# Chunked linear attention inside a one-core mixture block: chunks of 128 tokens made into chunks of 64

## The chip, the core and the metric

The kernel runs on one core of a Trainium2 chip. The metric is device time in microseconds of one launch, the median of several runs. Five engines work beside each other, each through its own queue in order: the PE (TensorE, matrix products; its weight loads have rows of their own, PEld), DVE (VectorE), ACT (ScalarE), POOL (GpSimd) and SP, which issues most transfers. PSUM, where matmul results land, has eight banks of 128 partitions by 512 float32 columns.

## The reference, cut to what matters

The input is 8 sequences (b = 0 to 7) of 512 tokens and 512 features. After a layer norm, one branch is a linear attention with 16 heads of 32 features, the other a mixture of 16 experts with 4 per token; the output is `x + attention * silu(mixture)`. In the attention each head has a decay `lam`, and the reference goes through the tokens in chunks of C = 128:

```
scores  = (q_i @ k_i^T) * D            # D[t,s] = exp(lam*(t-s)) for t >= s, else 0
o_intra = scores @ v_i
o_inter = (q_i * decay_q) @ S          # S: the state before the chunk, 32x32 a head
S       = lam_C * S + (k_i * decay_k)^T @ v_i
o       = o_intra + o_inter
```

Then o is multiplied with a sigmoid gate, each head is normalised by its root mean square, and a 512 by 512 product with Wo follows. The result of the recurrence does not depend on the size of the chunk.

## The kernel before, in words

All of it is float32. Heads come in four groups (g = 0 to 3) of four, so that a group fills 128 partitions. For one (b, g) the attention does this, with the lines of the profile:

- `key` and `query` (L659 products of 4 matmuls by 512 columns; ACT's Silu L669; four DVE operations L671 to L675 for the rotation) leave kT and qT, features on partitions, 512 tokens on columns. The key product goes to PSUM tag "m" (one bank), the query product to tag "d" (two banks).
- `by_token` transposes kT to tokens on partitions (L691, three chunks), into the one kept bank "k", and ACT scales it by the decay of the token (L696, four operations) into `kd`.
- `scores` makes the chunks' key-value products (L714, 12 matmuls of 128 rows by 32 columns, four column strips of the array beside each other), then the scores (L725, 16 matmuls of 32 rows, four row strips beside each other, each head in a bank of tag "a", 512 columns). DVE runs the state recurrence, multiplies qT by the decay into `qd` (L744), and masks the scores (L750, four operations of 512 columns) into `sc`.
- `output` adds the inter products and the intra products (L772, 16 matmuls, four column strips) in one bank of tag "d"; DVE multiplies it into the gate (L776).

The recurrence has two forms. For b below 2 it is three small DVE operations (L738, L740), and the inter products are 12 matmuls of 32 by 32 (L766). From b = 2 on it is one DVE scan over three states (L729); ACT copies the four heads' states into the diagonal blocks of a zeroed 128 by 128 tile (`blocked`, L734, four copies), and the inter products are 3 full matmuls (L761).

A float32 matmul has two weight loads and two matmul records in the trace, so 16 matmuls are "x32".

The order around it is written out by hand in `sequence`: for each g, scores(g); key(g+2) or, for g of 2 and 3, the value products of the next sequence, value(b+1, 2(g-2)); by_token(g+1); projections of the sequence before (L817, tag "d"); query(g+2) or value(b+1, 1); then output(g). After output(3): gate_2 of the next sequence (L645, four banks "a"), value(b+1, 3), `squares` (ACT L783 squares each group, the PE sums them, L786), key and query of the next sequence, `normed` (L805, L810). Value products (L615, copied out by ACT at L619) use bank "m" for even t and "d" for odd t. The `on_pe` blocks keep the PE in the order in which the program is written; other engines are ordered by the scheduler. In the first stage `along` puts pieces of the router and of the shared expert between these steps: share_1 writes its gate product to bank "m" (L355), share_2 its third tile (L371). From b = 2 on `advance` puts steps of the mixture between them: gathers and adds on POOL, and DVE operations L1354, L1358 and L1381, which wait for POOL in DVE's queue.

Scratch tiles: `sc` has four buffers, `kd` and `qd` have one each; the four squares use the buffers of `sc`.

Of the kernel before, what the change touches and what calls it, by code (L numbers as in the profile page):

```python
# [10 lines left out]
F32 = mybir.dt.float32  # L11
# [11 lines left out]
G, HG = 4, 4  # L23
C = 128
NC = N // C
NT = B * NC
KC = D // P
E, F, TOPK = 16, 128, 4
# [25 lines left out]
def shape_constants():  # L54

    f = np.float32
    c = {}
    lam = -(f(2.0) ** (f(-8.0) * (np.arange(H, dtype=f) + f(1.0)) / f(H))).astype(f)
    i = np.arange(C, dtype=f)
    diff = i[None, :] - i[:, None]  # L60
    dec = np.exp(lam[None, :, None] * np.maximum(diff, f(0.0))[:, None, :])
    c["dmask"] = np.where(diff[:, None, :] >= 0, dec, f(0.0))
    dq = np.exp(lam[:, None] * (i[None, :] + f(1.0)))
    c["dq"] = np.repeat(dq.reshape(G, HG, 1, C), HD, axis=2).reshape(G, P, C).transpose(1, 0, 2)
    c["dk"] = np.exp(lam[None, :] * (f(C) - f(1.0) - i[:, None]))
    lc = np.exp(lam * f(C))
    c["lamc"] = np.repeat(lc.reshape(G, HG, 1), HD, axis=2).reshape(G, P).T

    c["carry"] = np.tile(c["lamc"][:, :, None, None] * (np.arange(NC - 1) > 0), (1, 1, HD, 1))
    half = HD // 2  # L70
    theta = (f(BASE) ** (f(-2.0) * np.arange(half, dtype=f) / f(HD))).astype(f)
    ang = (np.arange(N, dtype=f)[None, :] * theta[:, None]).astype(f)
    c["cos"] = np.tile(np.cos(ang), (2 * HG, 1))
    c["sin"] = np.tile(np.concatenate([-np.sin(ang), np.sin(ang)], axis=0), (HG, 1))
    c["ident"] = np.eye(P)


    sel = np.zeros((P, H - HG + Q))
    exp = np.zeros((H, G, P))
    for g in range(G):  # L80
        for j in range(HG):
            sel[j * HD : (j + 1) * HD, H - HG + j] = 1.0 / HD
            exp[g * HG + j, g, j * HD : (j + 1) * HD] = 1.0
    c["sel"] = sel

    c["tri"] = np.triu(np.ones((P, P)), 1) - 1.0
    c["iota_e"] = np.tile(np.arange(E), (P, 1))
    c["reset"] = np.tile((np.arange(NT) > 0)[None], (P, E)).reshape(P, E * NT)
    out = {k: np.ascontiguousarray(v.reshape(P, -1), dtype=f) for k, v in c.items()}
    out["exp"] = exp.reshape(H, D).astype(f)  # L90
    out["iota_b"] = (np.arange(P, dtype=f)[:, None] // Q * NBQ + np.arange(NBQ, dtype=f)).astype(f)
    out["token"] = (
        np.arange(NT)[None, :] * P + np.arange(P)[:, None] - B * N // 2).astype(np.float32)
    return out
# [3 lines left out]
def tile_block(ctx: ExitStack, tc: tile.TileContext, a: dict, out: bass.AP):  # L98
# [80 lines left out]
    cos = load(const, "cos", [P, N])  # L179
    sin = load(const, "sin", [P, N])  # L180
    wq = load_w(const, "wq")
    dk = load(const, "dk", [P, H])
    lamc = load(const, "lamc", [P, G])
    dq = load(const, "dq", [P, G, C])
    dmask = load(const, "dmask", [P, H, C])
    sel = load(const, "sel", [P, H - HG + Q])
    nw = load(const, "nw", [P, G])
    wo = load_w(const, "wo")
# [415 lines left out]

    between = [lambda: None]

    kept, carry, blocked = [], [], []

    def value(b, t):
        if t == 0:  # L610
# [73 lines left out]
    def by_token(b, g):  # L684

        if not kept:
            kept.append(bank("k", f"pk_{b}_{g}"))
        pk = kept[0]
        with on_pe():
            for c in range(NC - 1):  # L690
                nc.tensor.transpose(  # L691
                    pk[:, c * P : (c + 1) * P], kT_of[g][:, c * C : (c + 1) * C], ident)
        kd = scr[0].tile([P, NC - 1, HG, HD], F32, tag="kd", name=f"kd_{b}_{g}")
        by_chunk = pk[:, : (NC - 1) * P].rearrange("p (c h d) -> p c h d", c=NC - 1, d=HD)
        for j in range(HG):
            nc.scalar.activation(  # L696
                kd[:, :, j, :], by_chunk[:, :, j, :], AF.Copy,
                scale=dk[:, g * HG + j : g * HG + j + 1])
        kd_of[g] = pk[:, (NC - 1) * P :], kd

    masked = []

    def scores(b, g):

        pkv, kd = kd_of.pop(g)
        states = pkv[:, : (NC - 1) * HD].rearrange(
            "p (e c) -> p c e" if carry else "p (c e) -> p c e", e=HD)
        with on_pe():  # L710
            for c in range(NC - 1):
                for j in range(HG):
                    h = g * HG + j
                    nc.tensor.matmul(  # L714
                        states[j * HD : (j + 1) * HD, c, :], lhsT=kd[:, c, j, :],
                        rhs=v_of[b][:, c, h * HD : (h + 1) * HD], start=True, stop=True)
        kT, qT = kT_of.pop(g), qT_of.pop(g)
        sc_of[g] = []
        pss = [bank("a", f"ps_{b}_{g}_{j}") for j in range(HG)]
        with on_pe():  # L720
            for c in range(NC):
                cs = slice(c * C, (c + 1) * C)
                for j in range(HG):
                    hs = slice(j * HD, (j + 1) * HD)
                    nc.tensor.matmul(  # L725
                        pss[j][:, cs], lhsT=kT[hs, cs], rhs=qT[hs, cs], start=True, stop=True)
        st = scr[0].tile([P, (NC - 1) * HD], F32, tag="state", name=f"state_{b}_{g}")
        if carry:
            nc.vector.tensor_tensor_scan(  # L729
                st, carry[0][:, g, :], pkv[:, : (NC - 1) * HD], 0.0, ALU.mult, ALU.add)  # L730
            st_of[g] = blocked[g % 2]
            for j in range(HG):
                hs = slice(j * HD, (j + 1) * HD)
                nc.scalar.copy(  # L734
                    st_of[g][hs, :, hs], st[hs].rearrange("p (e c) -> p c e", e=HD))
        else:
            st_of[g] = st = st.rearrange("p (c e) -> p c e", e=HD)
            nc.vector.tensor_copy(st[:, 0], states[:, 0])  # L738
            for c in range(1, NC - 1):
                nc.vector.scalar_tensor_tensor(  # L740
                    st[:, c], st[:, c - 1], lamc[:, g : g + 1], states[:, c],
                    ALU.mult, ALU.add)
        qd = scr[0].tile([P, NC - 1, C], F32, tag="qd", name=f"qd_{b}_{g}")
        nc.vector.tensor_tensor(  # L744
            qd, qT[:, C:].rearrange("p (c t) -> p c t", t=C),
            dq[:, g].unsqueeze(1).to_broadcast([P, NC - 1, C]), ALU.mult)
        qd_of[g] = qd
        for j in range(HG):
            s = scr[0].tile([P, NC, C], F32, tag="sc", name=f"sc_{b}_{g}_{j}", bufs=4)
            masked[:] = [nc.vector.tensor_tensor(  # L750
                s, pss[j].rearrange("p (c t) -> p c t", t=C),
                dmask[:, g * HG + j].unsqueeze(1).to_broadcast([P, NC, C]), ALU.mult).ins]
            sc_of[g].append(s)

    def output(b, g):
        po = bank("d", f"po_{b}_{g}")
        st, qd, sc = st_of.pop(g), qd_of.pop(g), sc_of.pop(g)
        with on_pe():
            for c in range(1, NC):
                if carry:  # L760
                    nc.tensor.matmul(  # L761
                        po[:, c * C : (c + 1) * C], lhsT=st[:, c - 1, :], rhs=qd[:, c - 1, :],
                        start=(c == 1), stop=False)
                for j in range(0 if carry else HG):
                    hs = slice(j * HD, (j + 1) * HD)
                    nc.tensor.matmul(  # L766
                        po[hs, c * C : (c + 1) * C], lhsT=st[hs, c - 1, :], rhs=qd[hs, c - 1, :],
                        start=(c == 1), stop=False)
            for c in range(NC):
                for j in range(HG):  # L770
                    h = g * HG + j
                    nc.tensor.matmul(  # L772
                        po[j * HD : (j + 1) * HD, c * C : (c + 1) * C],
                        lhsT=v_of[b][:, c, h * HD : (h + 1) * HD],
                        rhs=sc[j][:, c], start=False, stop=(c == NC - 1))
        nc.vector.tensor_tensor(on_of[b][:, g, :], po, on_of[b][:, g, :], ALU.mult)  # L776


    def squares(b):
        pr = bank("a", f"pr_{b}")  # L780
        for g in range(G):
            sq = scr[0].tile([P, N], F32, tag="sc", name=f"sq_{b}_{g}", bufs=4)
            nc.scalar.activation(sq, on_of[b][:, g, :], AF.Square)  # L783
            with on_pe():
                for c in range(NC):
# [48 lines left out]
    def experts_of_blocks():  # L834
# [1 line left out]
        work = scr[0].tile([P, 2, NBQ], F32, tag="state", name="work")  # L836
        ef, ei = work[:, 0], work[:, 1].bitcast(I32)
        for i in range(0, NBQ, some):
            cm = scr[0].tile([P, some, 2 * E], F32, tag="sc", name=f"cm_{i}", bufs=4)
            with behind(DVE):  # L840
                nc.vector.tensor_tensor(
                    cm, end.rearrange("p w e -> p (w e)").unsqueeze(1).to_broadcast(
# [577 lines left out]
        last(b, t, m_of.pop((b, t)), pw)  # L1420

    scr[0] = scr2
    carry.append(load(comb, "carry", [P, G, HD * (NC - 1)]))
    for j in range(2):
        blocked.append(comb.tile([P, NC - 1, P], F32, tag=f"blocked{j}", name=f"blocked{j}"))
        nc.gpsimd.memset(blocked[j], 0.0)
    other.append(comb)
    enter(FIRST, ps=ahead[0])
    for b in range(FIRST, B):
# [63 lines left out]
```

## Time and profile before

| | |
|---|---|
| median of 3 runs | 1138.0 us (1137.63 to 1138.36) |
| the profiled execution's own time | 1134.81 us |
| its span on the core | 1133.0 us |
| busy PE, DVE, ACT, POOL | 1106.5, 737.3, 428.6, 447.2 us |
| router, shared expert, attention of b = 0 and 1 | to about 300 us |
| experts by blocks | about 300 to 690 us |
| attention of b = 2 to 7 with the mixture | about 690 us to the end |

The page lists busy time by engine, then the span in 40 slices with the busy share in tenths, then groups of instructions. A row of the timeline has the start, the busy time of a run of equal instructions, the engine, the line, what is written and read, and the count. Busy time on the PE counts matmuls in flight, so it is read together with the waits: who waited for whom, total, times, longest.

### The profile page before, as it was taken

How to read it: one execution, taken by the hardware profiler on the slowest of the kernel's cores; microseconds unless marked ns; L12 is line 12 of the kernel's file. 1: busy time of each engine (PE TensorE's matmuls, PEld its weight loads, DVE VectorE, ACT ScalarE, POOL GpSimd, SP SyncE). 2: the span in 40 equal slices, each digit the busy share in tenths (PEclk: the TensorE clock that was granted, in tenths of full speed). 3: DMA queues.
4: the chain of work that ended last, by engine and by line, in shares of the span. 5: the costliest groups of instructions: out<-in, count | busy, mean ns of one | idle time of the engine just before them, and what ended most of it. 6: DMA issues, size and time to landing. Idle time of an engine off the chain costs nothing. (4 is left out here: it accounts for less than half of the span.)

```text
span 1133.0 us, 21299 instructions
## 1 busy us (share of the span) xinstructions
PE 1106.5 (98%) x7670; PEld 675.5 (60%) x7670; DVE 737.3 (65%) x1584; ACT 428.6 (38%) x924; POOL 447.2 (39%) x430
## 2 busy tenths in 40 slices
PE   7999999998999999999999999999999999999998
PEld 4445554455577777777777775655645555546453
DVE  6357744899344455444445446968889597797774
ACT  3223424264443333333333442353442522523541
POOL 4212100200333333333333323855877858858211
PEclk9999999999999999999999999999999999999999
DMA  9995342092789999989999975824647537444012
GB/s 341 326 319 191 143 151 48 22 383 70 239 201 234 244 236 241 240 237 239 237 240 249 256 204 216 292 81 142 232 121 236 177 113 258 143 136 142 19 38 75
DMA packets 163930, 218.48 MB, mean 193 GB/s; under 512 B 89840, under 2 KB 99184, under 8 KB 161776
## 3 DMA queue, kind: packets, MB, share of 16 engines
q1 hardware_dynamic: 142704, 146.76, 41.6%
q0 software_dynamic: 21120, 70.34, 23.4%
q8 instruction: 63, 1.03, 0.4%
q14 instruction: 43, 0.35, 0.1%
HBM read 126.78 MB, written 72.43 MB: 176 GB/s over the span
## 5 line engine op out<-in xcount | busy, mean ns | idle before, releaser
L1224 PE MATMUL pgu<-xts,wst 128*128 128x256 f32 x896 | 202.6, 379 | 0.0
L1224 PEld LDWEIGHTS pgu<-xts,wst 128*128 128x128 f32 x896 | 170.1, 190 | 46.2 <-issue 13.2
L1343 POOL DMA_INDIRECT yg<-y_d,place x128 | 142.8, 1115 | 30.3 <-issue 18.3
L1153 POOL DMA_INDIRECT more<-xn_d,slot x69 | 65.6, 951 | 216.6 <-DVE w L1207 113.8
L1255 PE MATMUL py<-wexp,slb 128*128 x272 | 129.9, 593 | 0.0
L1259 DVE TENSOR_SCALAR y<-py,w 128x512 f32<-128x512 f32 x136 | 102.0, 750 | 41.5 <-PE py L1255 34.8
L615 PE MATMUL pv<-wv,xT 128*128 128x512 f32 x256 | 118.2, 602 | 1.0 <-ACT sh L374 1.0
L659 PE MATMUL pk<-xT,wk 128*128 128x512 f32 x256 | 118.2, 603 | 0.0
L659 PE MATMUL pq<-xT,wq 128*128 128x512 f32 x256 | 115.7, 593 | 0.3 <-PEq L1307 0.3
L1236 ACT ACTIVATE slb<-pgu 128x256 f32<-128x256 f32 (+1 forms) x80 | 28.2, 352 | 222.7 <-PE pgu L1224 180.6
L1237 DVE TENSOR_TENSOR slb<-slb,pgu 128x256 f32<-128x256 f32 (+1 forms) x80 | 30.5, 381 | 121.1 <-ACT slb L1236 121.1
L817 PE MATMUL pw<-wo,on 128*128 128x512 f32 x224 | 100.6, 596 | 5.2 <-DVE m L1381 4.4
L1153 POOL DMA_INDIRECT xg<-xn_d,slot x67 | 63.7, 950 | 101.4 <-DVE w L1207 48.2
L1385 POOL TENSOR_TENSOR xo<-xo,m 128x512 f32<-128x512 f32 x31 | 45.3, 1462 | 128.1 <-DVE m L1381 120.9
L1186 ACT COPY xts<-pl 128x512 uint16<-128x512 uint16 x110 | 84.3, 769 | 2.4 <-DMA pl<-more 1.3
L750 DVE TENSOR_TENSOR sc<-ps,dmask 128x512 f32<-128x512 f32 x128 | 79.0, 676 | 1.0 <-PE ps L725 1.0
L659 PEld LDWEIGHTS pq<-xT,wq 128*128 128x128 f32 x256 | 47.2, 190 | 54.2 <-issue 52.7
L615 PEld LDWEIGHTS pv<-wv,xT 128*128 128x128 f32 x256 | 46.0, 190 | 51.3 <-issue 46.8
L659 PEld LDWEIGHTS pk<-xT,wk 128*128 128x128 f32 x256 | 46.2, 189 | 50.7 <-issue 48.3
L817 PEld LDWEIGHTS pw<-wo,on 128*128 128x128 f32 x224 | 41.2, 190 | 54.5 <-issue 45.2
L1205 DVE COPY wst<-wexp 128x512 f32 x112 | 43.2, 426 | 37.0 <-DVE y L1259 15.7
L1255 PEld LDWEIGHTS py<-wexp,slb 128*128 128x128 f32 x272 | 45.5, 191 | 27.4 <-issue 26.8
(196 smaller groups left out, 1713.1 us busy)
## 6 DMA issues: line engine op xcount, KB each, us to landing
y_d<-y SPq DMA_DIRECT2D x136, 256.0 KB, 4.1
wexp<-in_experts SPq DMA_DIRECT2D x16, 768.0 KB, 5.0
sh_d<-sh SPq DMA_DIRECT2D x32, 256.0 KB, 3.5
xT<-xT_d SPq DMA_DIRECT2D x8, 1024.0 KB, 6.7
m<-sh_d SPq DMA_DIRECT2D x32, 256.0 KB, 4.6
xo<-in_x SPq DMA_DIRECT2D x32, 256.0 KB, 2.8
out<-xo SPq DMA_DIRECT2D x31, 256.0 KB, 2.0
x<-in_x SPq DMA_DIRECT2D x7, 1024.0 KB, 8.8
```

What stands on the lines that cost most here:

```text
L615: nc.tensor.matmul(pv, lhsT=xT_of[b][:, k, t * P : (t + 1) * P], rhs=wv[:, k, :], start=(k == 0), stop=(k == KC - 1))
L659: nc.tensor.matmul(ps, lhsT=w[:, k, g * P : (g + 1) * P], rhs=xT_of[b][:, k, :], start=(k == 0), stop=(k == KC - 1))
L750: masked[:] = [nc.vector.tensor_tensor(s, pss[j].rearrange("p (c t) -> p c t", t=C), dmask[:, g * HG + j].unsqueeze(1).to_broadcast([P, NC ...
L817: nc.tensor.matmul(pw, lhsT=on_of[b][:, g, t * P : (t + 1) * P], rhs=wo[:, g, :], start=(g == 0), stop=(g == G - 1))
L1153: nc.gpsimd.indirect_dma_start(out=row(i), out_offset=None, in_=xn_d, in_offset=bass.IndirectOffsetOnAxis(ap=slot[:, i : i + 1], axis=0))
L1186: (nc.vector.tensor_copy if j in by_dve else nc.scalar.copy)(xt[:, u, KP:, :].bitcast(U16).rearrange("p k (t h) -> p h k t", h=2), pls[j % ...
L1205: nc.vector.tensor_copy(to, wflat[:, bass.ds(off + u * KC * F, KC * F)])
L1224: nc.tensor.matmul(pg[:, o * 2 * P : (o + 1) * 2 * P], lhsT=wst[j % 2][k // KP][:, (k % KP * 2 + o) * F :][:, :F], rhs=xt[:, :, k, :], sta ...
L1255: nc.tensor.matmul(py, lhsT=hT[:, u * P : (u + 1) * P], rhs=wflat[:, bass.ds(off + KC * 2 * F, D)], start=True, stop=True)
L1259: gone.append(nc.vector.tensor_scalar(y, py, w[:, u : u + 1], None, ALU.mult).ins)
L1343: nc.gpsimd.indirect_dma_start(out=yg, out_offset=None, in_=y_d, in_offset=bass.IndirectOffsetOnAxis(ap=place[:, r, g : g + 1], axis=0))
L1385: nc.gpsimd.tensor_tensor(xo, xo, m, ALU.add)
```

## The change

Chunks have 64 tokens (S = 64, NS = 8), and the form is the same for all b.

- Two chunks share a 128-token tile. `by_token` transposes all four tiles; ACT scales each head twice, for the first and for the second half of a tile (`dk` has zeros for the other half): eight operations in place of four. The key-value products are 7 chunks by 4 heads, 128 rows by 32 columns, as before.
- Scores of a chunk are 64 by 64: 32 matmuls of 32 rows and 64 weight columns; odd chunks go to the upper 64 PSUM partitions, so that a head's scores take 256 columns.
- One scan over seven states serves all b; the diagonal blocks, their copies, their memsets and the three small operations go. The inter products are 28 matmuls of 32 by 32 with 64 columns.
- The intra products are 32 matmuls of 64 rows and 32 weight columns with 64 columns.
- `output` writes even chunks to a bank of tag "d" and odd chunks to the bank of tag "m". DVE multiplies in two operations of 256 columns.
- `sc` tiles have 256 columns, so the squares (and a small comparison tile) use the single buffers of `kd` and `qd` in turn.

```
-            for c in range(NC - 1):
+            for t in range(NC):
                 nc.tensor.transpose(...)
...
+        for r in range(2):
+            for j in range(HG):
+                h = r * H + g * HG + j
+                nc.scalar.activation(
+                    kd[:, r::2, j, :], by_tile[:, : NC - r, j, :], AF.Copy, scale=dk[:, h : h + 1])
...
-            for c in range(NC):
+            for c in range(NS):
+                r = c % 2 * S
                 for j in range(HG):
                     nc.tensor.matmul(
-                        pss[j][:, cs], lhsT=kT[hs, cs], rhs=qT[hs, cs], start=True, stop=True)
+                        pss[j][r : r + S, c // 2 * S : (c // 2 + 1) * S],
+                        lhsT=kT[hs, cs], rhs=qT[hs, cs], start=True, stop=True)
...
+        nc.vector.tensor_tensor_scan(st, carry[:, g, :], pkv, 0.0, ALU.mult, ALU.add)
...
-        po = bank("d", f"po_{b}_{g}")
+        pos = [bank("dm"[r], f"po_{b}_{g}_{r}") for r in range(2)]
...
+            for c in range(1, NS):
+                for j in range(HG):
+                    nc.tensor.matmul(
+                        pos[c % 2][hs, c // 2 * S : (c // 2 + 1) * S],
+                        lhsT=st[hs, c - 1, :], rhs=qd[hs, c - 1, :], start=(c < 3), stop=False)
+            for c in range(NS):
+                r = c % 2 * S
+                for j in range(HG):
+                    nc.tensor.matmul(
+                        pos[c % 2][j * HD : (j + 1) * HD, c // 2 * S : (c // 2 + 1) * S],
+                        lhsT=v_of[b][r : r + S, c // 2, h * HD : (h + 1) * HD],
+                        rhs=sc[j][r : r + S, c // 2], start=False, stop=(c >= NS - 2))
+        for r, po in enumerate(pos):
+            on = on_of[b][:, g, :].rearrange("p (c r t) -> p r c t", r=2, t=S)[:, r]
+            nc.vector.tensor_tensor(on, po[:, : NC * S].rearrange(...), on, ALU.mult)
...
-            sq = scr[0].tile([P, N], F32, tag="sc", name=f"sq_{b}_{g}", bufs=4)
+            sq = scr[0].tile([P, N], F32, tag=("kd", "qd")[g % 2], name=f"sq_{b}_{g}")
```

More of the change, by code (lines that the diff above doesn't have):

```diff
@@ L25 @@
 NC = N // C
+S = C // 2
+NS = N // S
 NT = B * NC
@@ L58, in shape_constants @@
     lam = -(f(2.0) ** (f(-8.0) * (np.arange(H, dtype=f) + f(1.0)) / f(H))).astype(f)
-    i = np.arange(C, dtype=f)
+    i = np.arange(S, dtype=f)
     diff = i[None, :] - i[:, None]
     dec = np.exp(lam[None, :, None] * np.maximum(diff, f(0.0))[:, None, :])
-    c["dmask"] = np.where(diff[:, None, :] >= 0, dec, f(0.0))
+    c["dmask"] = np.tile(np.where(diff[:, None, :] >= 0, dec, f(0.0)), (2, 1, 1))
     dq = np.exp(lam[:, None] * (i[None, :] + f(1.0)))
[L64 to L69, printed above, removed]
+    c["dq"] = np.repeat(dq.reshape(G, HG, 1, S), HD, axis=2).reshape(G, P, S).transpose(1, 0, 2)
+    dk = np.exp(lam[None, :] * (f(S) - f(1.0) - i[:, None]))
+    c["dk"] = np.kron(np.eye(2), dk).reshape(P, 2, H)
+    lc = np.exp(lam * f(S))
+    lamc = np.repeat(lc.reshape(G, HG, 1), HD, axis=2).reshape(G, P).T
+    c["carry"] = np.tile(lamc[:, :, None, None] * (np.arange(NS - 1) > 0), (1, 1, HD, 1))
     half = HD // 2
@@ L181, in tile_block @@
     wq = load_w(const, "wq")
[L182 to L185, printed above, removed]
+    dk = load(const, "dk", [P, 2 * H])
+    carry = load(const, "carry", [P, G, HD * (NS - 1)])
+    dq = load(const, "dq", [P, G, S])
+    dmask = load(const, "dmask", [P, H, S])
     sel = load(const, "sel", [P, H - HG + Q])
@@ L605, in tile_block @@
     between = [lambda: None]
-    kept, carry, blocked = [], [], []
+    kept = []
     def value(b, t):
@@ L689, in by_token @@
         with on_pe():
-            for c in range(NC - 1):
+            for t in range(NC):
                 nc.tensor.transpose(
[L692 to L699, printed above, removed]
+                    pk[:, t * P : (t + 1) * P], kT_of[g][:, t * C : (t + 1) * C], ident)
+        kd = scr[0].tile([P, NS - 1, HG, HD], F32, tag="kd", name=f"kd_{b}_{g}")
+        by_tile = pk.rearrange("p (t h d) -> p t h d", t=NC, d=HD)
+        for r in range(2):
+            for j in range(HG):
+                h = r * H + g * HG + j
+                nc.scalar.activation(
+                    kd[:, r::2, j, :], by_tile[:, : NC - r, j, :], AF.Copy,
+                    scale=dk[:, h : h + 1])
+        kd_of[g] = pk[:, : (NS - 1) * HD], kd
     masked = []
@@ L707, in scores @@
         pkv, kd = kd_of.pop(g)
-        states = pkv[:, : (NC - 1) * HD].rearrange(
-            "p (e c) -> p c e" if carry else "p (c e) -> p c e", e=HD)
+        states = pkv.rearrange("p (e c) -> p c e", e=HD)
         with on_pe():
-            for c in range(NC - 1):
+            for c in range(NS - 1):
                 for j in range(HG):
@@ L715, in scores @@
                         states[j * HD : (j + 1) * HD, c, :], lhsT=kd[:, c, j, :],
-                        rhs=v_of[b][:, c, h * HD : (h + 1) * HD], start=True, stop=True)
+                        rhs=v_of[b][:, c // 2, h * HD : (h + 1) * HD], start=True, stop=True)
         kT, qT = kT_of.pop(g), qT_of.pop(g)
@@ L720, in scores @@
         with on_pe():
-            for c in range(NC):
-                cs = slice(c * C, (c + 1) * C)
+            for c in range(NS):
+                cs = slice(c * S, (c + 1) * S)
+                r = c % 2 * S
                 for j in range(HG):
@@ L725, in scores @@
                     nc.tensor.matmul(
-                        pss[j][:, cs], lhsT=kT[hs, cs], rhs=qT[hs, cs], start=True, stop=True)
[L727 to L742, printed above, removed]
@@ L743, in scores @@
-        qd = scr[0].tile([P, NC - 1, C], F32, tag="qd", name=f"qd_{b}_{g}")
+                        pss[j][r : r + S, c // 2 * S : (c // 2 + 1) * S],
+                        lhsT=kT[hs, cs], rhs=qT[hs, cs], start=True, stop=True)
+        st = scr[0].tile([P, (NS - 1) * HD], F32, tag="state", name=f"state_{b}_{g}")
+        nc.vector.tensor_tensor_scan(st, carry[:, g, :], pkv, 0.0, ALU.mult, ALU.add)
+        st_of[g] = st.rearrange("p (e c) -> p c e", e=HD)
+        qd = scr[0].tile([P, NS - 1, S], F32, tag="qd", name=f"qd_{b}_{g}")
@@ L744, in scores @@
         nc.vector.tensor_tensor(
-            qd, qT[:, C:].rearrange("p (c t) -> p c t", t=C),
-            dq[:, g].unsqueeze(1).to_broadcast([P, NC - 1, C]), ALU.mult)
+            qd, qT[:, S:].rearrange("p (c t) -> p c t", t=S),
+            dq[:, g].unsqueeze(1).to_broadcast([P, NS - 1, S]), ALU.mult)
         qd_of[g] = qd
         for j in range(HG):
-            s = scr[0].tile([P, NC, C], F32, tag="sc", name=f"sc_{b}_{g}_{j}", bufs=4)
+            s = scr[0].tile([P, NC, S], F32, tag="sc", name=f"sc_{b}_{g}_{j}", bufs=4)
@@ L750, in scores @@
             masked[:] = [nc.vector.tensor_tensor(
-                s, pss[j].rearrange("p (c t) -> p c t", t=C),
-                dmask[:, g * HG + j].unsqueeze(1).to_broadcast([P, NC, C]), ALU.mult).ins]
+                s, pss[j][:, : NC * S].rearrange("p (c t) -> p c t", t=S),
+                dmask[:, g * HG + j].unsqueeze(1).to_broadcast([P, NC, S]), ALU.mult).ins]
             sc_of[g].append(s)
     def output(b, g):
-        po = bank("d", f"po_{b}_{g}")
+        pos = [bank("dm"[r], f"po_{b}_{g}_{r}") for r in range(2)]
@@ L757, in output @@
         st, qd, sc = st_of.pop(g), qd_of.pop(g), sc_of.pop(g)
         with on_pe():
[L759 to L764, printed above, removed]
+            for c in range(1, NS):
+                for j in range(HG):
                     hs = slice(j * HD, (j + 1) * HD)
@@ L766, in output @@
                     nc.tensor.matmul(
-                        po[hs, c * C : (c + 1) * C], lhsT=st[hs, c - 1, :], rhs=qd[hs, c - 1, :],
-                        start=(c == 1), stop=False)
-            for c in range(NC):
+                        pos[c % 2][hs, c // 2 * S : (c // 2 + 1) * S],
+                        lhsT=st[hs, c - 1, :], rhs=qd[hs, c - 1, :],
+                        start=(c < 3), stop=False)
+            for c in range(NS):
+                r = c % 2 * S
                 for j in range(HG):
@@ L772, in output @@
                     nc.tensor.matmul(
[L773 to L776, printed above, removed]
+                        pos[c % 2][j * HD : (j + 1) * HD, c // 2 * S : (c // 2 + 1) * S],
[3 more added lines that the diff above has]
+            on = on_of[b][:, g, :].rearrange("p (c r t) -> p r c t", r=2, t=S)[:, r]
+            nc.vector.tensor_tensor(
+                on, po[:, : NC * S].rearrange("p (c t) -> p c t", t=S), on, ALU.mult)
     def squares(b):
@@ L838, in experts_of_blocks @@
         for i in range(0, NBQ, some):
-            cm = scr[0].tile([P, some, 2 * E], F32, tag="sc", name=f"cm_{i}", bufs=4)
+            cm = scr[0].tile([P, some, 2 * E], F32, tag=("kd", "qd")[i // some % 2], name=f"cm_{i}")
             with behind(DVE):
@@ L1422, in tile_block @@
     scr[0] = scr2
[L1423 to L1426, printed above, removed]
     other.append(comb)
```

## The prediction

> **What bounds the kernel now.** First the page: who is busy, and where.
>
> ```profile
> PE 1106.5 (98%) x7670; PEld 675.5 (60%) x7670; DVE 737.3 (65%) x1584; ACT 428.6 (38%) x924; POOL 447.2 (39%) x430
> ...
> PE   7999999998999999999999999999999999999998
> ...
> DVE  6357744899344455444445446968889597797774
> ```
>
> The PE is full in every slice, DVE at most in the first and last third, where the attention lies. "Busy" on the PE counts matmuls in flight, so the waits decide whether it paces the kernel:
>
> ```profile
> PE pw L817 <- DVE m L1381: 4.4, 4, 1.9
> PE pn L565 <- DVE sc L750: 3.1, 2, 2.3
> ...
> PE psT L289 <- DVE sc L750: 1.0, 1, 1.0
> ...
> PE pl L318 <- DVE sc L750: 0.8, 1, 0.8
> ...
> PE pk L691 <- DVE state L729: 0.4, 1, 0.4
> ```
>
> These are all the waits of the PE for the work that the change makes lighter or moves: 9.7 us of a span of 1133.0. So the PE's own queue, in its written order, sets the end, and whatever makes the PE wait adds to it. Next, one pass of it in the last stage (b = 3), from the timeline:
>
> ```profile
> 797.75 0.50 PE L761 MATMUL po<-qd,blocked 128*128 128x128 f32 x3
> 798.18 1.08 PE L772 MATMUL po<-sc,v 128*32 128x128 f32 x32
> 799.08 0.37 PE L714 MATMUL pk<-v,kd 128*32 128x32 f32 x24
> 799.38 1.17 PE L725 MATMUL ps<-qT,kT 32*128 32x128 f32 x32
> 800.48 3.70 PE L615 MATMUL pv<-wv,xT 128*128 128x512 f32 x8
> ...
> 807.78 0.83 PE L761 MATMUL po<-qd,blocked 128*128 128x128 f32 x6
> ...
> 808.54 1.08 PE L772 MATMUL po<-sc,v 128*32 128x128 f32 x32
> ```
>
> Start to start is what a burst costs the queue: L761 0.76 (807.78 to 808.54), L772 0.90, L714 0.30, L725 1.10: 3.06 us for a (b, g). The single records behind these rows start in fours, 5 to 7 ns apart, one for each strip of the array; a four follows the last after 112 ns in L725 and 109 in L772 (128 columns), after 31.7 in L714 (32 columns). A change of strip shape costs about 0.1 us each side (L659 to L714 523 ns where matmul to matmul is 429; L725's last to the next matmul 200).
>
> **The PE's work.** 64 columns are not in the trace. Between 31.7 ns at 32 columns and 109 at 128, a straight line gives 58 ns for one set of strips. Scores: 64 records, eight strips, 8 sets x 58 = 0.46 plus 0.24 for entry and exit: 0.70, now 1.10. Intra: 0.46 + 0.20 = 0.66, now 0.90 (the exit to L714, today free since both have column strips, is a change of shape). Inter: 56 records on four diagonal tiles, 14 x 58 = 0.81 + 0.24 = 1.05, now 0.76. Key-value products: 8 more sets of 31.7, +0.25: 0.55. One more transpose: +0.11 (109 ns start to start). Sum 3.07 against 3.06 for the 24 (b, g) from b = 2. For b below 2 the inter burst L766 stands at 0.78 (115.11 to 115.89), so the sum is the same. I take 0 us in all. Whether eight strips run at once is not shown; bounds: eight at a time as above, or four, which makes intra and scores 16 sets each, 2 x 0.46 x 32 = +30 us. I take eight: in L714, L725 and L772 every strip that has its own weights runs beside the others, at the 5 to 7 ns spacing, and 8 x 6.7 = 54 ns fits in the 58.
>
> The Trainium skill, "TensorE: Matmul & The Clock Gate", Part 3 on packing small matmuls, has 16 tiles at 10.6 times one; at that efficiency (an estimate) a set of eight would be 88 ns and the sum +15 us. The section "Wait — 56ns, not 53.3ns?" of the same page speaks against the change: starts never come closer than about 25 ns; 240 records would then take 6.0 us a (b, g), some +90 us. The rows above have 5 to 7 ns across strips, so the floor can hold only for one strip (31.7).
>
> **The squares.** Now all four squares have buffers, and the PE finds them ready:
>
> ```profile
> 815.50 0.83 PE L761 MATMUL po<-qd,blocked 128*128 128x128 f32 x6
> 815.71 0.59 ACT L619 COPY v<-pv 128x512 f32<-128x512 f32 x1 [0.80 <-PE pv L615]
> ...
> 817.78 2.17 ACT L783 ACTIVATE sq<-on 128x512 f32<-128x512 f32 x4
> ...
> 822.01 1.08 PE L786 MATMUL pr<-sq,sel 128*32 128x128 f32 x32
> 823.02 1.55 PE L659 MATMUL pk<-xT,wk 128*128 128x512 f32 x3
> ```
>
> After the change square 2 takes the buffer of square 0 and may be written only when the PE has summed that one; in the PE's queue that sum stands behind value(n, 3). The chain from 822.0: sums of groups 0 and 1, 0.5 with latency; ACT's copy of the value (0.59, from 0.3 to 0.9) stands before square 2 in ACT's queue; squares 2 and 3, 0.61 and 0.52 more, to 2.05; sum of group 3 and exit, 0.4: key(n, 0) starts at about 2.4 and not at 1.0. Behind the waiting sum stands everything the PE has. 1.37 x 7 (b = 0 to 6) = +9.6 us; bounds 0.9 (no copy before it) and 2 (a table load of 1.28 between): 6 to 14.
>
> **The bank "m".** Two waits. First, at g = 3 output follows value(n, 2), which also fills "m"; the first inter matmul writes the odd chunk's bank. The rows above: value ends, L761 starts at 815.50; the copy that empties "m" runs 815.71 to 816.30. So +0.9 for b = 2 to 6, 4.6 us (for b = 0 and 1 other matmuls lie between, b = 7 has no value). Second, after every output the next user of "m" waits for both DVE multiplies:
>
> ```profile
> 116.90 3.70 PE L371 MATMUL pys<-sw,h 128*128 128x512 f32 x8
> ...
> 120.82 0.68 DVE L776 TENSOR_TENSOR on<-po,on 128x512 f32<-128x512 f32 x1
> ```
>
> ```profile
> 726.49 2.84 PE L615 MATMUL pv<-wv,xT 128*128 128x512 f32 x6
> ...
> 727.70 0.68 DVE L776 TENSOR_TENSOR on<-po,on 128x512 f32<-128x512 f32 x1
> ```
>
> In the first, the third tile of L371 (116.90 + 1.72) uses "m" and will wait to about 121.65: 3.0; the other outputs of b = 0 add 0.8 and 0.3: 4.1. In the second, value(3, 0) is due at 726.5 and the second multiply ends near 728.5 or later. Going through all L776 ends against the next "m" matmul for b = 2 to 7, with 1.05 us of cover by key-value products and scores: g = 0 gives 0.5, 0, 0.15, 2.9, 0.15, 0.45, g = 1 gives 2.1, 1.3, 0.2, 0, 0, g = 2 nothing (gate_1 covers it); 7.8 in all. DVE is lighter by then (below), but `qd` and the last rotation now stand before the multiply in its queue; I take 5.4, bounds 2 and 11. b = 1 by the same count has 5.5, with the table work on DVE; there the lighter masks take away the 3.1 of L565, and DVE catches up while the PE waits: I take 0 net, bounds -3 and +4.
>
> **DVE and ACT.** A mask goes from 512 to 256 columns. L744 with 384 takes 0.55, L750 with 512 takes 0.68, so about 1 ns a column: -0.27 x 4. Scan of 224 for 96: +0.15; `qd` +0.06; second multiply +0.15. DVE loses about 0.7 us a (b, g). On the path that is worth only waits: psT and pl for the masks, -0.8 of 1.8. ACT gets four more scalings (+1.1 us; L696 starts are 0.22 apart) and loses four copies L734 (1.3) from b = 2. The scaling is covered: it has the 3.43 us of a query or value product, and ended 2.1 us (836.5 to 838.58) before L714 needed it; uncovered it would be 1.1 x 8 = 9 us in b = 0, 1. The waits for L1381 and L729 (4.8) come from POOL's adds ahead in DVE's queue; with the PE held elsewhere by more than that in each b, they go: -4.8. SP loses one small load and carries 0.15 MB less; POOL loses two memsets; neither is waited for.
>
> **Sum** against the profiled execution: 0 + 9.6 + 4.6 + 4.1 + 5.4 - 4.8 - 0.8 = +18.1. 1134.8 + 18.1 = 1152.9; the median lies 3.2 above the profiled time, so about 1156 us.
>
> **Rivals.** *Eight strips do not run, or are not fed.* Output and scores now follow each other as 240 short records. The longest such chain in the trace has 120 (734.56 to 737.98, 28 ns each); 24 of them in a row ran at 8 ns. Four at a time costs +30: 1185; a feed that gives one record in 28 ns would cost 3.7 us in each of 21 such chains: +78, 1233. For it: nothing shows 13 ns held over 240. Against: a semaphore record of L761 at 737.25 shows the PE's sequencer past the 19 large records after L725 while half of L725 was still to start, so the supply ran ahead. Chance 0.16, mostly at 1175 to 1190. *Only the waiting strip waits* (faster): in the trace's L725 at 736.9 three strips went on while the fourth waited for its bank. If the PE lets ready matmuls of the next product pass a held sum or a held "m" matmul, all new waits (23.7) vanish and the 9.7 us of old ones too: 1138 - 9.7 = 1128. It decides if L786's third sum is passed by key(n, 0). Against: L817, whole arrays, held everything for 1.9 us. Chance 0.11. *The holds are short*: the "m" waits after output and in b = 0 fall to their covers and the squares to 0.9: +2 to +6, 1140 to 1144. Chance 0.07.
>
> **The numbers.** Forecast 0.66 (1146 to 1168), not eight or fed too slowly 0.16, short holds 0.07, passing 0.11. The range 1143 to 1186 leaves out the passing case, half of the short holds and the worst of the feed. 0.2% (2.3 us) is about what a measurement can tell: faster 0.10 and same 0.02 (of the passing case, a little of it and of the short holds ends near 1138), slower 0.88.
>
> **What would show it.** Right: the sums of a b in two pieces with ACT's square between, 1.4 us; output(3) 0.9 after the value; waits of the PE for DVE's multiply at key, value and the shared expert's third tile; scores and intra bursts near 0.7 start to start; L1381 gone from the waits. Wrong: bursts of 64 records at 1 us or more (the feed), or dense matmuls between the sums (passing).

## The result: 1206.8 us, slower by 6%

The changed kernel takes 1206.8 us (1204.9 to 1210.5, four runs) against 1138.0 before (1137.6 to 1138.4): ratio 1.060, interval 1.058 to 1.062. The forecast was 1156 with a range to 1186. The profiled execution is the slowest of the four: 1210.5 us with a span of 1208.7, +75.7 on the 1133.0 of before (the medians differ by 68.8).

Two rows of the page of the changed kernel show where to look, the granted clock in tenths by slice and the PE's instruction queue:

```profile
PEclk9999999999999999999999999998998999989999
...
q8 instruction: 98, 1.61, 0.6%
```

The same row of the DMA queues of the kernel before (packets, MB, share of 16 engines):

```profile
q8 instruction: 63, 1.03, 0.4%
```

Every packet of q8 has 16384 bytes. The page counts 24,460 records of PE and PEld now and 15,340 before; with those of the PE's sequencer (semaphores, registers, branches) the trace has 25,000 and 15,882. At one packet for 256 instructions the 98 and 63 packets hold 25,088 and 16,128: they fit the PE's program. Next, the PE's waits of the changed kernel (total us, times, longest):

```profile
PE ps L731 <- issue: 16.1, 9, 2.6
PE pk L719 <- issue: 12.1, 6, 3.9
...
PE pk L663 <- DVE on L770: 5.2, 3, 2.6
PE pr L781 <- ACT sq L778: 4.3, 7, 0.6
PE pv L619 <- DVE on L770: 2.7, 2, 1.5
PE pg L359 <- DVE on L770: 1.7, 1, 1.7
PE pys L375 <- DVE on L770: 1.6, 1, 1.6
```

L719 is the key-value product (L714 before), L731 the scores (L725), L756 and L764 inter and intra, L770 DVE's multiply, L781 the sums of the squares. The first two rows had no counterpart: the PE stands in the middle of short products and waits for nothing that the profile shows. One such place, from the timeline:

```profile
832.65 0.56 PE L719 MATMUL pk<-v,kd 128*32 128x32 f32 x41
836.82 0.44 PE L719 MATMUL pk<-v,kd 128*32 128x32 f32 x15 [3.61 <-issue]
837.20 1.48 PE L731 MATMUL ps<-qT,kT 32*64 32x64 f32 x64
838.61 5.47 PE L619 MATMUL pv<-wv,xT 128*128 128x512 f32 x8
```

A burst stands for 3.6 us after 41 of its 56 records; then the eight records of a value product take 5.47 us instead of 3.70. The last is the clock, as two windows of the same place show (window, length, busy PE, PEld, DVE, ACT and POOL with counts, granted clock, DMA share, GB/s):

```profile
828.00:832.00 4.00, 4.00 (x80) 2.02 (x85) 3.79 (x5) 0.13 (x1) 3.74 (x3) 1.00 0.99 331
...
836.00:840.00 4.00, 3.18 (x81) 2.44 (x81) 2.15 (x6) 0.00 (x0) 3.31 (x4) 0.50 0.86 273
```

From b = 2 on the trace has 14 gaps of over 0.6 us in the PE's records that have no releaser and are not merely the spacing at half clock (one of 0.86 us at 710.05 is left aside; the kernel before has it too, at 693.51). Counting all records of the PE's queue from the start, its sequencer's included, each of the 14 begins where the count leaves 224 on division by 256; the three earlier ones (251, 284 and 297 us) all leave 193. So the PE runs out at the edge of an instruction block. At all 14 a q8 packet starts 2.3 to 2.8 us before the PE goes on. That packet starts 0.7 to 3.5 us after the PE has entered the block before; what delays it no run here shows.

The 75.7 us by cause:

| cause | us | from |
|---|---|---|
| PE out of instructions | 30.9 | waits on "issue": L731 16.1, L719 12.1, L619 1.5, L781 1.2 |
| half clock behind standstills and one wait | about 17 (an estimate) | 34 gaps between large matmuls, most 0.85 instead of 0.43: 14; the rest for short records in the same windows |
| waits for DVE's multiply in bank "m" | 11.2 | waits on L770, four rows |
| squares | 8.0 | L781 2.15 instead of 1.01, seven times |
| clean length of the bursts | 9 | 3.69 us a (b, g) instead of 3.41 for the five bursts listed below, x 32 |
| old waits gone (L1381, L750 at L565) | -7.5 | 4.4 and 3.1 |
| rest, gaps too short to assign | about 7 | difference |

Clean lengths are start to start in bursts without a wait: transposes 0.44 (before 0.33), key-value 0.63 (0.30), scores 0.84 (1.10), inter 1.00 (0.78), intra 0.79 (0.90).

### The profile page after: what moved, and what is told of

Same layout as the page of the kernel before. It is cut to its first block, busy times and chain, and to the rows that moved or that the text cites. A ratio compares the mean times of both kernels' runs of the same rounds, so it can differ in the third digit from the quotient of the medians.

```text
span 1208.7 us, 30476 instructions
## 1 busy us (share of the span) xinstructions
PE 1143.2 (95%) x12230; PEld 690.8 (57%) x12230; DVE 707.4 (59%) x1600; ACT 430.7 (36%) x956; POOL 439.6 (36%) x428
## 5 line engine op out<-in xcount | busy, mean ns | idle before, releaser
L1338 POOL DMA_INDIRECT yg<-y_d,place x128 | 135.8, 1061 | 58.6 <-PE pq L663 31.0
L619 PE MATMUL pv<-wv,xT 128*128 128x512 f32 x256 | 126.1, 635 | 4.9 <-DVE on L770 2.7
L663 PE MATMUL pk<-xT,wk 128*128 128x512 f32 x256 | 125.5, 634 | 5.2 <-DVE on L770 5.2
L1231 ACT ACTIVATE slb<-pgu 128x256 f32<-128x256 f32 (+1 forms) x80 | 28.2, 352 | 206.5 <-PE pgu L1219 183.2
L663 PEld LDWEIGHTS pk<-xT,wk 128*128 128x128 f32 x256 | 48.9, 201 | 60.0 <-issue 52.8
L619 PEld LDWEIGHTS pv<-wv,xT 128*128 128x128 f32 x256 | 48.8, 201 | 59.6 <-issue 52.9
L673 ACT ACTIVATE sk<-pk 128x512 f32<-128x512 f32 x32 | 19.1, 596 | 136.1 <-PE pk L663 128.2
L702 ACT ACTIVATE kd<-pk,dk 128x128 f32<-128x128 f32 (+1 forms) x256 | 66.3, 374 | 0.0
```

Of the source, the lines that this page charges most:

```text
L619: nc.tensor.matmul(pv, lhsT=xT_of[b][:, k, t * P : (t + 1) * P], rhs=wv[:, k, :], start=(k == 0), stop=(k == KC - 1))
L663: nc.tensor.matmul(ps, lhsT=w[:, k, g * P : (g + 1) * P], rhs=xT_of[b][:, k, :], start=(k == 0), stop=(k == KC - 1))
L702: nc.scalar.activation(kd[:, r::2, j, :], by_tile[:, : NC - r, j, :], AF.Copy, scale=dk[:, h : h + 1])
L1338: nc.gpsimd.indirect_dma_start(out=yg, out_offset=None, in_=y_d, in_offset=bass.IndirectOffsetOnAxis(ap=place[:, r, g : g + 1], axis=0))
```

## Experiments

The theory ("supply"): the PE's instructions come in blocks of 256; the next is usable only some 3 to 4.5 us after the one before was entered, and output and scores in a row are 480 instructions in 3.3 us. Rivals: short matmuls on eight strips stall by themselves ("shape"); other transfers hold the packet; DVE is late.

### Half a block more ahead

```
+    pad = bank("d", "pad")
+    with on_pe():
+        for i in range(32):
+            hs = slice(i % HG * HD, (i % HG + 1) * HD)
+            nc.tensor.matmul(
+                pad[hs, :HD], lhsT=ident[hs, hs], rhs=ident[hs, hs], start=True, stop=True)
     enter(FIRST, ps=ahead[0])
```

> The changed kernel with 32 more matmuls of 32 by 32 (128 instructions of the PE with their weight loads) put into the PE's queue once, before the first key product of b = 2; nothing reads their result. Supply theory: the PE takes its instructions from blocks of 256 (one 16384-byte packet of the instruction queue q8), the next block can be used 3.0 to 4.5 us after the one before was entered, and a burst that uses 256 instructions sooner stands still at the block's edge. Moving everything by half a block moves the stalls: the key-value products and scores that stood for 1.5 to 3 us near 814, 833 to 836, 900 (in the scores), 922 (in the scores) and 1166 (in the scores) go through clean or stall at another place (by the count of 256: in the scores at 837, 941, 988, 1007, 1094 and 1149, in the key-value products at 899, 921, 1019, 1068 and 1165). The number of stalls (about 20) and their sum (33 us) stay, so the time stays within 10 us of 1207. Rival (shape theory: bursts of eight strips stall by themselves, from banks or weight loads): the stalls stay in the same bursts of the same (b, g). Rival (transfers: the packet is late because other transfers of that moment hold it): the stalls stay at the same moments too.

Measured: 1210.2 us, one run. The place shown above, in this kernel's timeline:

```profile
835.34 0.70 PE L719 MATMUL pk<-v,kd 128*32 128x32 f32 x56
835.97 0.78 PE L731 MATMUL ps<-qT,kT 32*64 32x64 f32 x49
839.68 0.37 PE L731 MATMUL ps<-qT,kT 32*64 32x64 f32 x15 [2.93 <-issue]
```

The key-value burst is whole and the scores break: 128 instructions earlier in the program than the place of the stall before, modulo 256. Of the eleven new places named, ten came (not the one at 1068), and six more that were not named; the chain that stood at 815 in the changed kernel is clean; the remainder is 224 again at every one. The three stalls ahead of the pad (251, 284, 297) stayed where they were. Where a stall comes is thus set by the count of instructions, not by a burst and not by a moment's traffic. Their sum did not stay: the waits on "issue" are 40.9 us for 30.9, while those on L770 fell from 11.2 to 5.0, and the time came out 3.4 us higher.

### Very long chains

```
-            for c in range(NS - 1):              # key-value; the scores likewise at (5, 1)
+            for c in list(range(NS - 1)) * (20 if (b, g) == (3, 1) else 1):
```

> The changed kernel with two very long chains: in (b, g) = (3, 1) the key-value products are sent 20 times (2240 instructions of the PE, four strips), in (5, 1) the scores 20 times (2560 instructions, eight strips); the results are the same ones written again. By the pace of one burst the chains take 20 x 0.50 = 10 us and 20 x 0.70 = 14 us. Supply theory: from the second block on every 256 instructions take 3.0 to 4.5 us, with a stall at each edge: 28 to 38 us and 32 to 43 us, nearly the same per instruction (12 to 17 ns) in both shapes, with one packet of q8 for each 256 instructions. Shape theory: the four strips run through at 10 us, the eight strips stall: 14 to 40 us.

Measured: 35.8 us for the key-value products (810.42 to 846.19) and 39.3 for the scores (1013.82 to 1053.09). Two successive blocks of each, from the timeline:

```profile
830.58 1.93 PE L719 MATMUL pk<-v,kd 128*32 128x32 f32 x128 [1.80 <-issue]
834.31 1.93 PE L719 MATMUL pk<-v,kd 128*32 128x32 f32 x128 [1.80 <-issue]
...
1032.75 2.26 PE L731 MATMUL ps<-qT,kT 32*64 32x64 f32 x128 [1.49 <-issue]
1036.49 2.25 PE L731 MATMUL ps<-qT,kT 32*64 32x64 f32 x128 [1.49 <-issue]
```

Exactly 128 matmul records (with their loads 256 instructions), then a standstill. Settled, a block takes 3.5 to 4.0 us in both shapes (the first few up to 5.4). Four strips or eight make no difference: the shape theory falls, and the price is measured, some 3.7 us for 256 instructions, 58 ns for a float32 matmul of four instructions. It is a price at half clock: the granted clock was 0.50 from 817.6 to 851.7 and from 1019.0 to 1056.6, all through the settled blocks. A block has 1.9 or 2.3 us of work even so; the rest is standstill. Other transfers were few there: the DMA engines were busy to 0.27 and 0.24 (810 to 846 and 1014 to 1053), against 0.99 and 0.92 around the stall at 836.8. The instruction queue q8 has 116 packets, 18 more than in the changed kernel, for 4560 more instructions (17.8 blocks).

### The kernel before with a longer chain

```
-            for c in range(NC - 1):              # key-value products of the kernel before
+            for c in [c for _ in range(5) for c in range(NC - 1)]:
```

> The kernel before with each key-value product sent five times in place of once (the same result is written again): four strips at a time, 128 rows by 32 columns, no new wait and no eight strips. The extra work is 4 x 0.25 us in each of 32 bursts, 32.5 us: 1171 us. Supply theory: the chain of output and scores has 380 instructions in place of 188, 240 of them in 1.5 us; some 16 stalls of 1 to 2 us, 23 to 30 us in all, at edges of blocks of 256, and half-clock windows behind some of them: 1195 to 1215. Shape theory (the stalls belong to eight strips or to 64 columns): none, 1171.

Measured: 1169.9 us, one run. By the time alone the shape theory would have it; the trace says otherwise. The PE's waits of this kernel have two rows that the kernel before has not:

```profile
PE pk L714 <- issue: 9.2, 8, 2.2
...
PE ps L725 <- issue: 3.6, 2, 1.9
```

Of these 12.8 us one stall of 2.2 lies at 247 us; the others from b = 2 on, nine gaps, are all at block edges (remainder 224), in four-strip shapes of the old kernel. The time came out low for three reasons: a burst of five grew by 0.86 us and not 1.0 (27.5 us in all), there were fewer stalls than expected, and hardly any half clock (mean 1.00); old waits also vanish behind them (L1381 4.4 to 0.8). The size I expected was too large by about half, the mechanism holds.

### The chain cut

```
+            if g == 0 and b not in on_of:
+                gate_2(b)
+            output(b, g)
             if g + 2 < G:
                 query(b, g + 2)
...
-            if g == 0 and b not in on_of:
-                gate_2(b)
...
-            output(b, g)
```

A second kernel has the same cut and, beside it, one projection in each g.

> The changed kernel with one thing moved: in each g of the sequences of b = 0 to 6 output(g) stands ahead of query(g+2) or value(b+1, 1), and the projections keep their places (two beside g = 0, two beside g = 1); same instructions, same buffers, the last sequence as written. It separates the cut of the chain from the spread of the projections. Supply theory: stalls without a releaser 33 to 10 us (those of the last sequence stay), half-clock loss 17 to 5, waits for the bank m 11.9 to 3, gate_2 of b = 0 waits 3 longer: about 1167 us, 1160 to 1177. Rival: most of the gain of the earlier order came from the spread projections: 1185 or more.

> The changed kernel with another order: in each g of the sequences of b = 0 to 6 output(g) stands ahead of query(g+2) (for g = 2 ahead of value(b+1, 1)) and not behind it, so that a product of 3.4 us lies between output(g) and scores(g+1); the projections of the sequence before go one to each g. All instructions are the same. Supply theory: the chain of 480 instructions falls into two of 240; by the count of blocks the stalls fall to about a third (33 to some 12 us), the half-clock windows behind them with them (17 to some 6 us), and the waits for DVE's multiply into the bank m (11.9 us) go, since query and scores cover them; a mask that is not ready may cost 3 us for g = 2: about 1170 us, 1160 to 1185. Shape theory: the stalls stay, only the waits for the bank go: 1195.

Measured: the cut alone 1180.3 us (ratio to before 1.034, 1.029 to 1.039), the cut with the projections spread 1181.8 (1.039, 1.036 to 1.041). Same instructions in another order, 26 us gone; the spread adds nothing. With the cut alone the waits on "issue" at L731 and L719 fall from 28.2 to 3.5 us, all in the last sequence, which keeps its order; the windows at half clock fall from 41 to 16 us. Not all of the gain is supply: the waits for L770 fall from 11.2 to 1.4 us. The cut alone ended above its range, the other at the upper end of its own, because a new wait came (rows of the cut alone):

```profile
PE pq L663 <- DVE m L1376: 5.2, 5, 2.0
...
PE p L649 <- ACT sgs L325: 3.7, 1, 3.7
PE ps L731 <- issue: 3.5, 2, 1.9
```

The query now follows output at once and needs the bank of tag "d" that a projection filled; DVE empties it late. (With the spread: 7.4.) Waits of gate_2 for ACT in b = 0 grew from 0.9 to 3.7.

### Own buffers for the squares

```
-            sq = scr[0].tile([P, N], F32, tag=("kd", "qd")[g % 2], name=f"sq_{b}_{g}")
+            tag = ("kd", "qd", "sq", "sq" if other else "kd")[g]
+            sq = scr[0].tile(
+                [P, N], F32, tag=tag, name=f"sq_{b}_{g}", bufs=2 if other and g > 1 else 1)
```

> The changed kernel with buffers of their own for the squares of groups 2 and 3 (for b = 0 and 1 for group 2), so that no square waits for a sum. The sums of a b go from 2.15 back to 1.01 us, 1.14 x 7 = 8.0 us: 1199 if all of it lies on the path. If the hold only hides other waits (ACT's, the block's edge): 1204 or more.

Measured: 1193.9 us, ratio 1.048 (1.045 to 1.050), 13 below the changed kernel; profiled spans 1198.4 and 1208.7. The waits for ACT at the sums fall from 4.3 to 0.4 us. From b = 2 on the sums of a b take 1.01 us again; b = 0 keeps 1.63, b = 1 has 2.54 with a stall at a block's edge in it; all seven together are 7.0 us shorter, and not 8.0. Why the gain is 10 to 13 was not settled; the two kernels were not timed side by side, and the stalls differ somewhat between them (L731 and L719 26.3 us for 28.2).

### All mends

Three kernels: the cut from b = 1 on and in the last sequence, own squares, the projection of g right behind scores(g); the same with the projection behind the query; the first with diagonal blocks again.

```
             scores(b, g)
+            project_tiles(before, [g])      # second kernel: behind second(g)
...
+            output(b, g)
+            if b: second(g)                 # query(g+2) or value(n, 1)
...
+            for c in range(1, NS) if blocked else ():              # third kernel
+                nc.tensor.matmul(pos[c % 2][:, c // 2 * S : (c // 2 + 1) * S],
+                    lhsT=st[:, c - 1, :], rhs=qd[:, c - 1, :], start=(c < 3), stop=False)
```

> The changed kernel with all mends together: from b = 1 on output(g) ahead of the second large product of g, in the last sequence too; the projection of g right behind scores(g), so that DVE has a large product of time before the next product needs its bank (in the run with the other order this wait cost 7.4 us); b = 0 in the written order; squares with buffers of their own. Supply theory with the other terms: the stalls of the PE without a releaser fall to 3 to 6 us, the half-clock windows to two or none, the squares to 1.01 us, the waits for the bank m to the 3.5 us of b = 0; what stays over the kernel before is the clean length of the bursts (3.69 us a (b, g) for 3.41, times 32: +9.0) less its old waits: 1150 us, 1144 to 1158. Rival: with the stalls gone DVE and POOL, which sit on the same work, become late and the waits for the multiplies of the projections come back: 1160 or more.

> The kernel with all mends, but the projection of g behind query(g+2) and ahead of scores(g+1), and not behind scores(g): the bank of tag d that it needs was filled by output(g), and the query now gives DVE's multiply 3.4 us to empty it. The 6.2 us of waits for DVE L770 at the projections go: 1159 us, 1155 to 1163; 20 us stay over the kernel before, in the clean lengths of the bursts (+9), where the bank m of the key product is still being emptied when output starts, and in b = 0. Rival: only 4 us of key and transposes then lie between scores and output, and DVE's masks come late: 1165 to 1175.

> The kernel with all mends, and from b = 2 on the inter products as 7 full matmuls of 128 by 128 with 64 columns from diagonal blocks (ACT copies the four heads' states into them, as the kernel before did) in place of 28 matmuls of 32 by 32. 84 instructions fewer a (b, g), and the burst by its columns 0.76 x 7 x 64 / (3 x 128) = 0.89 at most for 1.00: -0.11 to -0.17 x 24 = -2.6 to -4, and the rest of the stalls goes: 2 to 7 us below the run with all mends. Rival: with 64 columns the full weight load (128 by 128) sets the pace, or the copies come late: no gain, or up to 5 us slower.

Measured: 1165.4 us (ratio 1.022, 1.020 to 1.024); 1170.4 (1.026); 1177.4 (1.033). In the first the stalls are down to 3.8 us and the squares right, but projections wait 6.2 us for L770, where the time lies 7 us above the expected range. That is the rival's time, though the wait is for the multiply of output and not for those of the projections. The query between did not help: 8.0 us for L770, and 3.2 of output for ACT's Silu of the key (L673), which empties the bank. The rival's time came (1165 to 1175), its cause did not: no row has a wait of L756 or L764 for DVE's masks. The row that decides the third, an inter product from its timeline:

```profile
969.78 1.74 PE L759 MATMUL po<-qd,blocked 128*128 128x64 f32 x14
```

1.67 us to the next burst for 14 records, against 1.00 for the 56 small ones; 0.67 x 24 is 16 us. Inside the burst a record follows the last after 111.5 ns; with 128 columns (807.78 in the kernel before) after 112. I scaled by columns; a full array takes the same time with half of them. The rival had the pace right and the size wrong: 12 us slower than the first kernel, and not up to 5.

### The kernel before, projections spread

```
-        fill = ([0], [1], [2], [3], [], [], [], [])
+        fill = ([0], [], [1], [], [2], [], [3], [])
```

> The kernel before with one change of order: the four projections of the sequence before go one to each g and not two to g = 0 and two to g = 1. Its 4.4 us of waits for DVE L1381 (a projection waits for the bank of the last one) should go: 1134.5, 1132 to 1137. Rival: the waits move to another user of the tag d, as they did in the changed kernel with the other order: 1139 to 1146.

Measured: 1144.7 us, ratio 1.006 (1.004 to 1.008). The waits moved to inter and transposes (L761 for L1381 6.3, L691 for L729 3.7). No version here beats the kernel before.

## Why the prediction was wrong, point by point

- **The step that failed: "I take 0 us in all" for the PE's work, and the case that I put beside it.** "Eight strips do not run, or are not fed" had 0.16, "mostly at 1175 to 1190". The second half of it came true: 31 us of standstill and some 17 of half clock, and the working had no term for the second. I had priced the feed as a pace per record (28 ns); in truth records go freely as long as the block has come: 224 in 2.8 us at 1147.06, over an edge (1148.68) whose packet had started early. The bill comes at the edge of a block that is late. My argument against it, that the PE's sequencer was past 19 large records at 737.25, showed only that it runs ahead inside a block: by the count all of that lies in the block entered at 736.49 and left at 748.17.
- **Eight strips do run.** 64 score records start within 0.70 us, on average 87 ns for a set of eight. I had 58 from a straight line through rows with four strips. The sets are not even: in the burst at 795.83 they follow each other after 107, 58, 59, 68, 167, 79 and 67 ns. So the line's 58 is there, but two sets are much later; why, no run here shows. So scores cost 0.84 and not 0.70, intra 0.79 and not 0.66, key-value 0.63 and not 0.55; inter is 1.00 for my 1.05. Together 3.36 for my 3.07: +9 us that I put at 0.
- **The squares** cost 1.14 each, 8.0 in all, for 9.6. The timeline of the changed kernel has the two pieces with ACT between, and the next key product at 779.53 (2.15 after the first sum) where 1.01 would have been enough:

```profile
777.38 0.65 PE L781 MATMUL pr<-sq,sel 128*32 128x128 f32 x16
...
777.97 1.15 ACT L778 ACTIVATE sq<-on 128x512 f32<-128x512 f32 x2
...
778.65 0.94 PE L781 MATMUL pr<-sq,sel 128*32 128x128 f32 x16 [0.63 <-ACT sq L778]
```

- **The bank "m" behind output**: 11.2 for 9.5. b = 0 gave 3.3 (4.1 expected), b = 1 gave 1.5 (0), b = 2 to 7 gave 6.4 (5.4). Where a stall takes the PE's time such a wait disappears: with the pad, the waits of the key product at 736, 991 and 1151 are gone but for 0.2 us.
- **The bank "m" between value(n, 2) and output(3)**: inter and intra take 2.14 and not 1.79 us there, 0.36 each, 1.8 in all, for 4.6. The rows of the changed kernel:

```profile
770.50 0.59 PE L756 MATMUL po<-qd,state 32*32 32x64 f32 x24
771.03 0.31 PE L764 MATMUL po<-sc,v 64*32 64x64 f32 x6
771.27 0.71 PE L756 MATMUL po<-qd,state 32*32 32x64 f32 x32
```

  The 24 records of even chunks and six intra records stand ahead of the odd chunks, and while they run ACT's copy (770.61 to 771.20) empties "m". This is not the PE passing held matmuls: it is the order of the program. An `on_pe` block keeps its place in the queue, but inside it the scheduler orders, and for g = 3 of b = 2 to 6 it put the products in this order. The changed kernel and six of the runs with its parts have the same 24, 6, 32 and 58 records at all five places, starting about 0.52, 0.24 and 0.64 us after one another. So I had this term too large because I took the order as written. For "only the waiting strip waits" no row speaks: past a held sum of squares nothing went, and the three strips that I saw go on at 736.9 were the second records of matmuls that stand ahead of the held one (it starts at 736.895, the next matmul at 736.953).
- **Old waits**: the projection's wait for the multiply of m is gone, and the waits at the scores' masks fell, as the sum had it.

The Trainium skill, "Runtime: NRT & Kernel Launch", section "Instruction fetch mechanics", says that instructions come in 16 KiB blocks of 256, and that crossing one is mostly hidden since issue is slower than the refill. The block size agrees with the packets here. That it is hidden holds for the kernel before, where blocks are entered 7.7 us apart or more from the third stage on; in a chain that uses one in 2 us it does not.

The page "TensorE: Matmul & The Clock Gate", Part 3 on packing small matmuls, has 16 tiles at 10.6 times one; the estimate of 88 ns for a set of eight, which the prediction put aside, scaled my own 58 by it. The measured mean is 87 and not 58. But the sets are uneven, so one mean does not show that the efficiency of 16 tiles is what acts here.

## What to carry to other kernels

Count instructions, not only array time: where chains use 256 PE instructions (64 float32 matmuls with their loads) in less than about 4 us, expect the PE to stand at block edges. Not at every one: five blocks of the changed kernel from b = 2 on were used up in 1.7 to 2.6 us without a standstill, because the next packet had started before they were entered. A standstill is often paid again in half clock. Put a long product between bursts of short ones, so that no 256 instructions in a row are all short; the total per stage may stay as it is. The sign in a trace is an idle PE with "issue" as the releaser, in the middle of a burst, and at places that leave the same remainder when the records of the PE's queue are counted modulo 256.

## What the runs showed of the hardware

- In a chain of short matmuls one block of 256 PE instructions per 3.5 to 4.0 us was the settled pace, the same for four and for eight strips (at a granted clock of 0.50); a single stall let the PE go on 3.05 to 5.8 us after it had entered the block before.
- After seven of the ten standstills of over 1.6 us in the changed kernel, and after one wait of 2.75 us for DVE (736.4), the granted clock falls to 0.50 in windows of 3.4 or 6.8 us (41 us in all, 8 in the first kernel with all mends, the last window at the end of the span counted in both); 512-column records then start 0.85 us apart and not 0.43.
- Eight strips of 64 columns take 87 ns a set on average; a full 128 by 128 float32 record follows the last after 0.11 us with 64 columns as with 128.
